# Half of a kernel's last matrix products as four 64x64 parts, with a changed order of evictions and stores

## The chip, the core and the metric

The kernel runs on one core of a Trainium2 chip. The core has five engines with queues of their own: PE (TensorE, matrix products; the profile shows its weight loads apart, as PEld), DVE (VectorE), ACT (ScalarE), POOL (GpSimd) and SP (SyncE, which here only issues DMAs). Matrix products land in PSUM[...]. The results of a product are copied ("evicted") from PSUM to SBUF by ACT or DVE and stored to HBM by DMA. The metric is the device time of one execution in microseconds.

## The reference

An input x of shape (4, 256, 64, 64), float32, passes through two layers. The first computes attention over the 49 positions of a dilated 7x7 neighbourhood: a 7x7 convolution to 128 channels, a 1x1 convolution to 49, a softmax over the 49, and with these weights a sum of the 49 shifted copies of x. The second layer is the one that the change touches. It whitens the channels in four groups of 64:

```
x = transpose(X, (1, 0, 2, 3)).reshape(g, nc, -1)      # g = 4 groups, nc = 64 channels
xc = x - mean
Sigma = EPS * I + einsum('gdm,gem->gde', xc, xc) / m
Sigma_N = Sigma * rTr                                   # rTr = 1 / trace
P = I
for _ in range(5):
    P3 = P @ P @ P
    P = 1.5 * P - 0.5 * P3 @ Sigma_N
wm = P * sqrt(rTr)
X_hat = wm @ xc                                         # per group
return X_hat * weight + bias
```

The last product takes a 64x64 matrix for each group of channels. It is followed by a scale and a shift for each channel.

## The kernel before, in words

The 256 channels are held as two blocks of 128 partitions (`cc` 0 and 1), each with two groups of 64 channels. An image's rows are held in two slots, even rows and odd rows (`slots[2 * b + pr]` for image `b` and row parity `pr`), each of (128, 2, 32, 64) for partition, channel block, row and column.

Most of the time goes to the first layer. Its convolution is done by evaluation and interpolation (products at lines 502 and 608). Both lines write 49 outputs each into two halves of the PE array's columns: `h = 0` to PSUM partitions from 0, `h = 1` to partitions from 64. The attention sum is at line 955, its transposes are at lines 926 and 987, and the sums for the covariance are gathered on the way at line 1008. Three slots that were spilled to HBM come back at line 880, queued on SP behind the last load of the attention weights (`bring_back`).

Then follows `whiten` (lines 1185 to 1260), a short serial chain for each channel block. The two chains are run in turn, step by step. It forms the covariance, runs the iteration with products at lines 1231 and 1238 and vector steps at line 1241, and ends with a scale for each channel (line 1251) and a shift: a one-column product (line 1255), then lines 1258 and 1259. Its whitening matrix `wm[cc]` is 128x128, with the matrices of two groups on the diagonal and zeros in the two other quarters.

The last stage (lines 1267 to 1298) applies it. For each image (3, 2, 1, 0), channel block and block of 8 rows per parity (`q`, 0 to 3), two products of 128x128 by 128x512 are made (line 1276), one for each row parity, into PSUM tiles of one bank from a pool of three (`tp()`). They are evicted alternately by ACT (line 1287) and DVE (line 1291), which apply scale and shift and interleave the two parities into an output tile `st` of 16 rows. After the second eviction SP stores the tile, 128 partitions of 4 KB (line 1295). There are four such tiles. In all the stage has 64 products, 64 evictions and 32 stores of 512 KB.

Work stands on each engine's queue in the order that a scheduling layer gives it at build time. `pe(...)` keeps products in the order of the program, `tc.high_priority()` moves work ahead. Waits between engines are put in by the layer: for data, and for the reuse of a buffer. PSUM tiles of the stage are `tp` (three banks). Elsewhere in the kernel there are `ps_y` (two banks, the sums of line 955) and `cv_buf` (two banks, the convolution); both lie unused during the last stage.

Of the kernel before, what the change touches and what calls it, by code (L numbers as in the profile page):

```python
# [9 lines left out]
F32 = mybir.dt.float32  # L10
AF = mybir.ActivationFunctionType
ALU = mybir.AluOpType
# [19 lines left out]
def kernel(  # L32
# [29 lines left out]
    nc = tc.nc  # L62
    B, C, H, W = x.shape
    P = 128
# [5 lines left out]
    SH, SW = H // 2, W // 2  # L70
# [4 lines left out]
    GW = 64  # L75
# [15 lines left out]
    def pe(ins):  # L91
        return tc.keep_in_program_order(ins)

    const = ctx.enter_context(tc.tile_pool(name="const", bufs=1))
    work = ctx.enter_context(tc.tile_pool(name="work", bufs=2))
# [3 lines left out]
    ps_y = ctx.enter_context(tc.tile_pool(name="ps_y", bufs=1, space=bass.MemoryType.PSUM))  # L99
    ps_sg = ctx.enter_context(tc.tile_pool(name="ps_sg", bufs=1, space=bass.MemoryType.PSUM))  # L100

    def tp():
        return ps_tp.tile([P, 512], F32, tag="tp", name="tp")


    ident = const.tile([P, P], F32, name="ident")
# [15 lines left out]
    slots = {}  # L122
    store = []
# [27 lines left out]
    t = tp()  # L151
# [3 lines left out]
    t = tp()  # L155
    nc.tensor.matmul(t[:, :1], w2T, b1_sb, start=True, stop=True)
    bias = const.tile([P, 1], F32, name="bias")
    nc.vector.tensor_tensor(bias, t[:, :1], b2_sb, ALU.add)

    cv_buf = []  # L160
    for k in range(2):
        t = ps_cv.tile([P, 512], F32, name=f"cv{k}")
# [53 lines left out]
    for k, c0 in enumerate(range(0, P, CB)):  # L216
        n = min(CB, P - c0)
        t = cv_buf[k % 2]
        for cc in range(NCC):
# [5 lines left out]
                    start=True, stop=True,  # L225
# [8 lines left out]
    for k0 in range(0, KT, TB):  # L234
        n = min(TB, KT - k0)
        t = tp()
# [906 lines left out]
    for b in range(1, B):  # L1143

        steps = []
        for r in range(len(ROWS)):
            k = NR0 + len(ROWS) * (b - 1) + r
# [16 lines left out]
                j += 1  # L1164
    apool.release()
    rpool = ctx.enter_context(tc.tile_pool(name="rp", bufs=1, reuse_waits="tile"))
    blk = rpool.tile([P, P], F32, name="blk")
    nc.gpsimd.memset(blk, 0.0)
    for g in range(P // GW):
# [10 lines left out]
    def square(name):  # L1180
        return bpool.tile([P, P], F32, tag="xb", name=name, bufs=4)

    wm, sc, beta = {}, {}, {}

    def whiten(cc):


        def evict(o, i):
            (nc.vector.tensor_copy if cc else nc.scalar.copy)(o, i)

        G = sig[:, cc]
        mu = work.tile([P, 1], F32, tag="mu", name=f"mu{cc}")
        nc.vector.tensor_scalar(mu, G[:, GW : GW + 1], 1.0 / NPIX, None, ALU.mult)
        D = square(f"D{cc}")
        nc.vector.tensor_scalar(D, ident, mu, None, ALU.mult)
        t = tp()
        nc.tensor.matmul(t[:, :P], blk, D, start=True, stop=True)
        nmu = work.tile([P, 1], F32, tag="nmu", name=f"nmu{cc}")
        nc.vector.tensor_scalar(nmu, mu, -1.0, None, ALU.mult)
        PS = rpool.tile([P, 2, P], F32, tag="PS", name=f"PS{cc}", bufs=2)  # L1200
        S = PS[:, 1]
        nc.vector.tensor_scalar(S, ident, EPS, None, ALU.mult)
        yield
        for g in range(P // GW):
            gs = slice(g * GW, (g + 1) * GW)
            nc.vector.scalar_tensor_tensor(
                S[gs, gs], G[gs, :GW], 1.0 / NPIX, S[gs, gs], ALU.mult, ALU.add
            )
        nc.vector.scalar_tensor_tensor(S, t[:, :P], nmu, S, ALU.mult, ALU.add)
        yield  # L1210
        dt_ = square(f"dt{cc}")
        nc.vector.tensor_tensor(dt_, S, ident, ALU.mult)
        dg = work.tile([P, 1], F32, tag="dg", name=f"dg{cc}")
        nc.vector.tensor_reduce(dg, dt_, AX.X, ALU.add)
        t = tp()
        nc.tensor.matmul(t[:, :1], blk, dg, start=True, stop=True)
        yield
        rtr = work.tile([P, 1], F32, tag="rtr", name=f"rtr{cc}")
        nc.vector.reciprocal(rtr, t[:, :1])
        nc.vector.tensor_scalar(S, S, rtr, None, ALU.mult)  # L1220


        i15 = square(f"i15_{cc}")
        nc.vector.tensor_scalar(i15, ident, 1.5, None, ALU.mult)
        Pm = PS[:, 0]
        nc.vector.scalar_tensor_tensor(Pm, S, -0.5, i15, ALU.mult, ALU.add)
        yield

        for it in range(1, T_ITERS):
            t = tp()  # L1230
            nc.tensor.matmul(
                t[:, : 2 * P], Pm, PS.rearrange("p a c -> p (a c)"), start=True, stop=True
            )
            sq = rpool.tile([P, 2, P], F32, tag="sq", name=f"sq{cc}_{it}", bufs=2)
            evict(sq.rearrange("p a c -> p (a c)"), t[:, : 2 * P])
            yield
            t = tp()
            nc.tensor.matmul(t[:, :P], sq[:, 0], sq[:, 1], start=True, stop=True)
            nc.vector.tensor_scalar(Pm, Pm, 1.5, None, ALU.mult)
            yield  # L1240
            nc.vector.scalar_tensor_tensor(Pm, t[:, :P], -0.5, Pm, ALU.mult, ALU.add)
            yield


        q = work.tile([P, 1], F32, tag="q", name=f"q{cc}")
        nc.scalar.activation(q, rtr, AF.Sqrt)
        qi = work.tile([P, 1], F32, tag="qi", name=f"qi{cc}")
        nc.vector.reciprocal(qi, q)
        nc.vector.scalar_tensor_tensor(q, qi, rtr, q, ALU.mult, ALU.add)
        scale = work.tile([P, 1], F32, tag="scale", name=f"scale{cc}")  # L1250
        nc.vector.scalar_tensor_tensor(
            scale, q, 0.5, gain_sb[:, cc : cc + 1], ALU.mult, ALU.mult
        )
        t = tp()
        nc.tensor.matmul(t[:, :1], Pm, mu, start=True, stop=True)
        yield
        bt = work.tile([P, 1], F32, tag="beta", name=f"beta{cc}")
        nc.vector.tensor_scalar(bt, t[:, :1], scale, -1.0, ALU.mult, ALU.mult)
        nc.vector.tensor_tensor(bt, bt, shift_sb[:, cc : cc + 1], ALU.add)
        wm[cc], sc[cc], beta[cc] = Pm, scale, bt  # L1260

    chains = [whiten(cc) for cc in range(NCC)]
    for _ in itertools.zip_longest(*chains):
        pass


    NT = 512
    TR = NT // W
    n = 0
    for b in (3, 2, 1, 0):  # L1270
        for cc in range(NCC):
            for q in range(SH // TR):
                st = rpool.tile([P, TR, 2, W], F32, tag="out", name=f"out_{b}_{cc}_{q}", bufs=4)
                for pr in range(2):
                    t = tp()
                    nc.tensor.matmul(  # L1276
                        t,
                        wm[cc],
                        slots[2 * b + pr][:, cc, q * TR : (q + 1) * TR, :].rearrange(
                            "p r w -> p (r w)"  # L1280
                        ),
                        start=True,
                        stop=True,
                    )
                    t3 = t.rearrange("p (r w) -> p r w", w=W)
                    if n % 2 == 0:
                        nc.scalar.activation(  # L1287
                            st[:, :, pr, :], t3, AF.Identity, bias=beta[cc], scale=sc[cc]
                        )
                    else:  # L1290
                        nc.vector.tensor_scalar(  # L1291
                            st[:, :, pr, :], t3, sc[cc], beta[cc], ALU.mult, ALU.add
                        )
                    n += 1
                nc.sync.dma_start(
                    out[b, cc * P : (cc + 1) * P, 2 * q * TR : 2 * (q + 1) * TR, :],
                    st.rearrange("p r two w -> p (r two) w"),
                )


# [29 lines left out]
```

## Time and profile before

| | |
|---|---|
| time, median of 14 runs | 766.55 us (762.0 to 777.28) |
| the profiled execution | 777.28 us, of it 775.5 us span on the core |
| mean granted clock of PE in it | 0.977 of full speed |
| PE busy | 717.0 us, 92% of the span |
| DVE, ACT, POOL busy | 623.9, 326.6 and 34.2 us |
| first and last record of a product at L1276 | start at 715.64, end at 770.82 us |
| evictions at L1287 (ACT) and L1291 (DVE) | 32 of 778 ns, 32 of 810 ns |
| stores at L1295 | 32 of 512 KB, median 2.6 us from issue to landing |
| last store issued | 771.73 us |

The profile shows one execution. L1276 is line 1276 of the kernel. A group of instructions has its busy time, the mean duration of one, and the idle time of the engine before it with the work that ended the wait. A float32 product shows as two weight loads and two matmul records. The records of matmuls that follow each other overlap[...]: a record is longer than the distance to the next one. The profiled execution is the slowest of the runs listed.

### The profile page before, as it was taken

Reading aid. Unit: us, or ns where it says so; the run is one execution under the profiler, and the core shown is the slowest. Engines: PE = TensorE matmul, PEld = TensorE weight load, DVE = VectorE, ACT = ScalarE, POOL = GpSimd, SP = SyncE. Lnnn points to the kernel's source line nnn. Section 1 sums busy time; section 2 is a strip of 40 time slices with the busy share of each in tenths; the row PEclk is TensorE's granted clock in tenths of the full one; section 3 lists DMA queues with packets and bytes.
Section 4 is the critical chain, followed back from the end, with each engine's and each line's share of the span. In section 5 each row is a group of like instructions: output and inputs, shape, how many; then the busy total and the mean of one; then the engine's idle time right before and its main releaser. Section 6 shows DMA issues by size and latency. Waiting matters only on the chain.

```text
span 775.5 us, 18389 instructions
## 1 busy us (share of the span) xinstructions
PE 717.0 (92%) x7444; PEld 547.6 (71%) x7444; DVE 623.9 (80%) x1302; ACT 326.6 (42%) x950; POOL 34.2 (4%) x46
## 2 busy tenths in 40 slices
PE   6969989959899999989999999999999889998997
PEld 1429564345798888679988966898898678885443
DVE  2739999999899999998997799799979765535443
ACT  2403241025455465355453443735435563322443
POOL 0410000030000020001000100000000000000000
PEclk9998999989899999999999999999999999999999
DMA  8991020041744385045743930442532143381676
GB/s 321 229 320 40 31 106 37 1 153 38 226 140 138 117 307 161 19 128 204 255 126 94 342 81 1 141 116 96 161 87 79 48 143 114 100 306 48 275 309 282
DMA packets 59773, 114.76 MB, mean 148 GB/s; under 512 B 22903, under 2 KB 42024, under 8 KB 58920
## 3 DMA queue, kind: packets, MB, share of 16 engines
q1 hardware_dynamic: 55992, 94.71, 36.9%
q0 software_dynamic: 3696, 18.88, 7.2%
q8 instruction: 59, 0.97, 0.5%
q14 instruction: 26, 0.21, 0.1%
HBM read 66.23 MB, written 47.33 MB: 146 GB/s over the span
## 4 chain that ended last, share of the span: by engine, by line
DVE 39%; PE 35%; issue 4%; ACT 4%; DMA 3%; SPq 1%; DVEq 0%; ACTq 0%
PE y L955 11%; PE cv L502 8%; PE tp L1276 7%; DVE xh L307 5%; DVE pv L307 3%; DVE rb L307 3%; DVE zz L307 3%; DVE ct L307 3%; PE sig L1008 3%; DVE ct L300 3%; PE tp L926 3%; PE tp L987 3%; DVE rb L300 2%; DVE pv L303 2%; DVE band L908 2%
## 5 line engine op out<-in xcount | busy, mean ns | idle before, releaser
L502 PE MATMUL cv<-xh,wr 128*49 128x128 f32 x4368 | 254.2, 278 | 17.6 <-DVE xh L300 14.7
L502 PEld LDWEIGHTS cv<-xh,wr 128*49 128x49 f32 x4368 | 248.1, 125 | 22.8 <-issue 12.4
L955 PE MATMUL y<-band,xb 128*128 128x224 f32 (+2 forms) x640 | 153.3, 379 | 12.9 <-ACT xb L934 8.2
L955 PEld LDWEIGHTS y<-band,xb 128*128 128x128 f32 x640 | 111.1, 195 | 34.5 <-ACT xb L934 10.5
L512 ACT COPY pv<-cv 113x486 f32<-113x486 f32 (+1 forms) x63 | 29.8, 475 | 79.3 <-PE cv L502 78.1
L974 ACT ACTIVATE slot<-y,pivot 128x512 f32<-128x512 f32 x53 | 36.7, 738 | 58.8 <-PE y L955 58.8
L995 ACT COPY yt<-tp 128x256 f32<-128x256 f32 x128 | 45.5, 378 | 35.1 <-PE tp L987 34.1
L926 PE MATMUL tp<-ident,slot 128*128 128x128 f32 x256 | 50.5, 300 | 7.2 <-ACT yt L995 7.2
L987 PE MATMUL tp<-ident,slot 128*128 128x128 f32 x256 | 51.8, 298 | 4.0 <-ACT xb L934 1.4
L908 DVE STREAM_TRANSPOSE band<-band 128x960 f32<-128x960 f32 (+1 forms) x48 | 50.8, 1059 | 5.1 <-DMA band<-sd 5.0
L987 PEld LDWEIGHTS tp<-ident,slot 128*128 128x128 f32 x256 | 41.3, 205 | 13.9 <-issue 4.5
L926 PEld LDWEIGHTS tp<-ident,slot 128*128 128x128 f32 x256 | 40.1, 206 | 14.7 <-ACT yt L995 9.1
L1291 DVE TENSOR_SCALAR out<-tp,scale,beta 128x512 f32<-128x512 f32 x32 | 25.9, 810 | 29.5 <-PE tp L1276 29.5
L857 ACT COPY zt<-d 32x112 f32<-32x112 f32 (+2 forms) x156 | 45.0, 288 | 1.7
L811 ACT ACTIVATE d<-tp,mx 128x49 f32<-128x49 f32 x128 | 37.1, 338 | 15.1 <-DVE mx L806 15.0
L1287 ACT ACTIVATE out<-tp,beta,scale 128x512 f32<-128x512 f32 x32 | 24.9, 778 | 32.0 <-PE tp L1276 32.0
L934 ACT COPY xb<-tp 128x256 f32<-128x256 f32 x87 | 30.4, 377 | 17.6 <-PE tp L926 16.9
L307 DVE SCALAR_TENSOR_TENSOR xh<-ct 128x512 f32<-128x512 f32 x42 | 27.7, 682 | 12.4 <-PE cv L502 12.2
L1008 PE MATMUL sig<-yt 128*64 128x65 f32 x1024 | 36.9, 225 | 0.0
L1008 PEld LDWEIGHTS sig<-yt 128*64 128x64 f32 x1024 | 32.4, 137 | 6.0 <-issue 4.5
L1276 PE MATMUL tp<-slot,PS 128*128 128x512 f32 x80 | 35.9, 593 | 0.0
L608 PE MATMUL cv<-slot,wi 128*49 128x496 f32 (+3 forms) x168 | 34.8, 571 | 0.0
(206 smaller groups left out, 982.4 us busy)
## 6 DMA issues: line engine op xcount, KB each, us to landing
out_dram<-out SPq DMA_DIRECT2D x32, 512.0 KB, 2.6
sd<-zt SPq DMA_DIRECT2D x16, 896.0 KB, 3.9
slot<-in_x_dram POOLq DMA_DIRECT2D x12, 1024.0 KB, 9.8
band<-sd SPq DMA_DIRECT2D x128, 84.0 KB, 2.1
wr<-gd SPq DMA_DIRECT2D x15, 588.0 KB, 3.9
wr<-gd SPq DMA_DIRECT2D x15, 490.0 KB, 3.5
spill<-slot POOLq DMA_DIRECT2D x3, 2048.0 KB, 8.2
back<-spill SPq DMA_DIRECT2D x3, 2048.0 KB, 8.1
```

What stands on the lines that cost most here:

```text
L300: return in_turn(TT(o, a, b, ALU.add))
L307: return in_turn(STT(o, a, f, b, ALU.mult, ALU.add))
L502: nc.tensor.matmul(cv[h * HB : h * HB + KT, k, sr : sr + n, sc : sc + n], wv[:, sc, sr, cc], xh[bc][:, :n, h * NCC + cc, :n], start=(j == ...
L811: nc.scalar.activation(d[:, h, i], lt[i // NI][:, i % NI, h, :KT], AF.Exp, bias=mx[:, i, h : h + 1], accum_out=s[:, h, i : i + 1],)
L857: ins = nc.scalar.copy(o, i)
L908: nc.vector.transpose(f, f)
L926: nc.tensor.transpose(t[:, cc * P : (cc + 1) * P], xt[:, cc, CR * m : CR * (m + 1), bass.ds(pc, SW, 2)], ident,)
L955: nc.tensor.matmul(ps[:, cc, q0 - half * HALF : q1 - half * HALF, :], xb[:, cc * P : (cc + 1) * P], rhs, start=(k == 0), stop=(k == len(PI ...
L987: nc.tensor.transpose(t[:, cc * P : (cc + 1) * P], yt[:, cc, CR * i : CR * (i + 1), bass.ds(pc, SW, 2)], ident,)
L995: nc.scalar.copy(yb.rearrange("p a g c -> p (a g) c")[:, :, :GW], t[:, :C].rearrange("p (e c) -> p e c", c=GW),)
L1008: nc.tensor.matmul(sig[g * GW : (g + 1) * GW, cc], yb[:, cc, g, :GW], yb[:, cc, g], start=(count[0] == 0 and cc == 0), stop=(count[0] == 4 ...
L1276: nc.tensor.matmul(t, wm[cc], slots[2 * b + pr][:, cc, q * TR : (q + 1) * TR, :].rearrange("p r w -> p (r w)"), start=True, stop=True,)
```

## The change

The stage now works on two blocks of 8 rows at a time (16 groups of four products). Of the four products of a group, the two of even rows are made as before, one bank each, from `tp()`; call them plain(0) and plain(1). The two of odd rows use that `wm` has only two non-zero quarters: each product is split into two of 64x64 by 64x512, so that a group has four such parts, for the four quarters of the array. For `k = 0` a channel group's result lands on its own partitions. For `k = 1` the two groups are exchanged: channels 0 to 63 land on PSUM partitions 64 to 127 and the other way round, so that each part has a quarter of its own. The two results `ts[0]` and `ts[1]` lie in two banks, which are in turn the two of `ps_y` and the two of `cv_buf`.

`ts[0]` is evicted whole. `ts[1]` is evicted in two halves of 64 partitions, each to the other 64 partitions of the output tile; its scale and shift come from `abx`, which holds them in exchanged order. `abx` is made by one small product per channel block at the end of `whiten`, with a permutation matrix `swap` that POOL writes earlier. `n[0]` counts evictions over all groups and alternates ACT and DVE: five in a group. The first store of a group follows when its 16 output rows are complete, the second at the end of the group. Output tiles are six instead of four.

```diff
+    swap = rpool.tile([P, P], F32, name="swap")
+    for g in range(P // GW):
+        nc.gpsimd.tensor_copy(
+            swap[:, g * GW : (g + 1) * GW], ident[:, (1 - g) * GW : (2 - g) * GW]
+        )
     blk = rpool.tile([P, P], F32, name="blk")
...
-        scale = work.tile([P, 1], F32, tag="scale", name=f"scale{cc}")
+        ab = work.tile([P, 2], F32, tag="ab", name=f"ab{cc}")
+        scale = ab[:, 0:1]
...
-        bt = work.tile([P, 1], F32, tag="beta", name=f"beta{cc}")
+        bt = ab[:, 1:2]
         nc.vector.tensor_scalar(bt, t[:, :1], scale, -1.0, ALU.mult, ALU.mult)
         nc.vector.tensor_tensor(bt, bt, shift_sb[:, cc : cc + 1], ALU.add)
         wm[cc], sc[cc], beta[cc] = Pm, scale, bt
+        yield
+
+        t = tp()
+        nc.tensor.matmul(t[:, :2], swap, ab, start=True, stop=True)
+        abx[cc] = work.tile([P, 2], F32, tag="abx", name=f"abx{cc}")
+        nc.vector.tensor_copy(abx[cc], t[:, :2])
...
+    n = [0]
+
+    def out_rows(o, i, scale, bias):
+        n[0] += 1
+        if n[0] % 2:
+            nc.scalar.activation(o, i, AF.Identity, bias=bias, scale=scale)
+        else:
+            nc.vector.tensor_scalar(o, i, scale, bias, ALU.mult, ALU.add)
+
+    def two_banks():
+        while True:
+            t = ps_y.tile([P, 2, NT], F32, tag="y", name="apply")
+            yield [t[:, k] for k in range(2)]
+            yield cv_buf
+
+    G0, G1 = slice(0, GW), slice(GW, P)
+    two = two_banks()
     for b in (3, 2, 1, 0):
         for cc in range(NCC):
-            for q in range(SH // TR):
-                st = rpool.tile([P, TR, 2, W], F32, tag="out", name=f"out_{b}_{cc}_{q}", bufs=4)
-                for pr in range(2):
-                    t = tp()
-                    nc.tensor.matmul(t, wm[cc], ...)
...
+            for q in range(0, SH // TR, 2):
+                st = [
+                    rpool.tile([P, TR, 2, W], F32, tag="out", name=f"out_{b}_{cc}_{q + k}", bufs=6)
+                    for k in range(2)
+                ]
...
+                ts = next(two)
+
+                def plain(k):
                     t = tp()
+                    pe(nc.tensor.matmul(t, wm[cc], y[0][k], start=True, stop=True))
+                    out_rows(st[k][:, :, 0, :], rows_of(t), sc[cc], beta[cc])
...
+                plain(0)
+                for k in range(2):
+                    for i in (G0, G1):
+                        o = i if k == 0 else (G1 if i is G0 else G0)
+                        pe(
+                            nc.tensor.matmul(
+                                ts[k][o], wm[cc][i, i], y[1][k][i],
+                                start=True, stop=True, skip_group_check=True,
+                            )
                         )
...
+                out_rows(st[0][:, :, 1, :], rows_of(ts[0]), sc[cc], beta[cc])
+                store(0)
+                for i, o in ((G1, G0), (G0, G1)):
+                    out_rows(
+                        st[1][o][:, :, 1, :], rows_of(ts[1])[i], abx[cc][i, 0:1], abx[cc][i, 1:2]
+                    )
+                plain(1)
+                store(1)
```

More of the change, by code (lines that the diff above doesn't have):

```diff
@@ L1181, in square @@
         return bpool.tile([P, P], F32, tag="xb", name=name, bufs=4)
-    wm, sc, beta = {}, {}, {}
+    wm, sc, beta, abx = {}, {}, {}, {}
     def whiten(cc):
@@ L1268 @@
     TR = NT // W
-    n = 0
+    n = [0]
[11 more added lines that the diff above has]
+    G0, G1 = slice(0, GW), slice(GW, P)
@@ L1270 @@
+    two = two_banks()
     for b in (3, 2, 1, 0):
         for cc in range(NCC):
-            for q in range(SH // TR):
-                st = rpool.tile([P, TR, 2, W], F32, tag="out", name=f"out_{b}_{cc}_{q}", bufs=4)
-                for pr in range(2):
-                    t = tp()
[L1276 to L1283, printed above, removed]
-                    )
[L1285 to L1288, printed above, removed]
-                        )
[L1290 to L1298, printed above, removed]
@@ new lines, with store @@
+            for q in range(0, SH // TR, 2):
[3 more added lines that the diff above has]
+                ]
+                y = [
+                    [
+                        slots[2 * b + pr][:, cc, (q + k) * TR : (q + k + 1) * TR, :].rearrange(
+                            "p r w -> p (r w)"
+                        )
+                        for k in range(2)
+                    ]
+                    for pr in range(2)
+                ]
+                rows_of = lambda t: t.rearrange("p (r w) -> p r w", w=W)
+                ts = next(two)
+                def plain(k):
+                    t = tp()
+                    pe(nc.tensor.matmul(t, wm[cc], y[0][k], start=True, stop=True))
+                    out_rows(st[k][:, :, 0, :], rows_of(t), sc[cc], beta[cc])
+                def store(k):
+                    nc.sync.dma_start(
+                        out[
+                            b, cc * P : (cc + 1) * P, 2 * (q + k) * TR : 2 * (q + k + 1) * TR, :
+                        ],
+                        st[k].rearrange("p r two w -> p (r two) w"),
+                    )
+                plain(0)
[7 more added lines that the diff above has]
+                            )
+                        )
+                out_rows(st[0][:, :, 1, :], rows_of(ts[0]), sc[cc], beta[cc])
[3 more added lines that the diff above has]
+                        st[1][o][:, :, 1, :], rows_of(ts[1])[i], abx[cc][i, 0:1], abx[cc][i, 1:2]
+                    )
+                plain(1)
+                store(1)
```

## The prediction

> **What bounds the kernel now.** I read the chain that ended last first, then the timeline of its last stretch, then the sums of that stage, then the sizes of its instructions. The tail of the chain in order of time (start, us, engine, line):
>
> ```profile
> 708.11 1.74 PE tp L1231 x4
> 715.78 55.05 PE tp L1276 x128
> ```
>
> One stage, the 64 whitening products, is the last 55 us, and PE alone carries it. The waits and groups of that stage (busy us, mean ns, idle before it and who ended it):
>
> ```profile
> L1276 PE MATMUL tp<-slot,PS 128*128 128x512 f32 x80 | 35.9, 593 | 0.0
> L1291 DVE TENSOR_SCALAR out<-tp,scale,beta 128x512 f32<-128x512 f32 x32 | 25.9, 810 | 29.5 <-PE tp L1276 29.5
> L1287 ACT ACTIVATE out<-tp,beta,scale 128x512 f32<-128x512 f32 x32 | 24.9, 778 | 32.0 <-PE tp L1276 32.0
> L1276 PE MATMUL tp<-back,PS 128*128 128x512 f32 x48 | 22.1, 592 | 0.0
> ```
>
> PE is never idle; both evicting engines idle more than half the time, always for PE. A product is two records ("passes"): 80 + 48 = 128 for 64 products. Next, the sums of two windows: the reload of spilled slots, then this stage (last columns: PE clock, share of DMA, GB/s).
>
> ```profile
> 690.00:694.00 4.00, 3.69 (x31) 3.24 (x28) 1.87 (x4) 1.44 (x4) 0.00 (x0) 1.00 1.02 434
> 716.00:771.00 55.00, 54.82 (x128) 23.94 (x126) 25.49 (x35) 24.88 (x32) 0.00 (x0) 1.00 0.70 288
> ```
>
> The stores use 0.70 of the DMA engines; full load moved 434 GB/s. The clock is 1.00, so the stage scales to other executions. 55.0 us for 128 passes is 0.429 us a pass, 0.858 a product.
>
> Whether PE can do several small products at once, and what a change of array shape costs, is in the timeline of earlier stretches (start, duration):
>
> ```profile
> 28.73 0.32 PE L239 MATMUL tp<-ident,tapT 113*128 113x113 f32 x1 [0.17 <-ACT tap L214]
> 28.97 0.64 PE L608 MATMUL cv<-slot,tap 128*49 128x512 f32 x2
> ...
> 299.87 0.40 PE L502 MATMUL cv<-xh,wr 128*49 128x128 f32 x4
> 300.20 0.39 PE L987 MATMUL tp<-ident,slot 128*128 128x128 f32 x1
> ```
>
> At 28.97 two 512-column passes into two 64-column halves of the array ran inside 0.64 us, 7 ns apart. The page's L608 row (168 passes, 34.8 us busy) says the same: 0.207 us a pass for a mean of 488 columns, half of what one array-wide pass needs. So two column halves run fully side by side, both passes of each. The switch: the 113-column pass at 28.73 streams for 113/512 x 0.429 = 0.095 us, yet the next starts 0.246 later; before other L502 groups it is 0.106 beyond the stream. I take 0.11 going in. Coming back, the last L502 pass starts at 299.99 (0.40 us record less its 0.275), streams 0.107, and L987 starts at 300.20: 0.10.
>
> [...] Nothing in this trace splits the array by rows[...]. [...]
>
> **The change, part by part.** The changed stage has 16 groups of four products: plain(0), two products as four 64x64 parts, plain(1).
>
> *PE per group.* plain(0): 2 x 0.429 = 0.858. Switch in 0.106. Four parts, if at once: 2 passes, 0.858, plus 3 starts of 7 ns, plus 0.04 since the first pass after a switch shows its weight load (467 against 429 ns between the first two L608 pairs): 0.918. Switch out 0.098. plain(1): 0.858 + 0.084, the delay of the second pass that the first L1276 product shows (513 against 429 ns). Sum 2.922 us instead of 4 x 0.858 = 3.433. The parts save 0.86 of 3.43, the switches give back 0.33. Sixteen groups: 46.75 instead of 54.93 us, **-8.2**. The switch costs for the 64x64 shape aren't in the trace: between nothing (5.3 us better) and twice (5.3 worse); I take the column-half values, the nearest.
>
> *Before the stage.* In the compiled order both swap products stand ahead of the first plain product in PE's queue and wait for beta. Now the first L1276 starts at 715.64; L1259 ends at 716.10 and 716.23. Then 0.05 to PE, two one-column products at the 0.22 us that L1255 took before the next weights, and weights: first product at about 716.64, **+1.0**. All 64 products queue behind it. The two abx copies (about 0.2 us each) end before DVE's first eviction. The swap tile costs POOL two copies; POOL is empty in this stage, they can run some 90 us earlier. Uncovered they would cost a fraction of a us. The larger pool leaves the three reloads on SP with the same waits.
>
> *Evictions.* 80 instead of 64. In the compiled order over two groups A and B, ACT does A plain(0), A plain(1), A first half, B ts[0], B second half; DVE does A ts[0], B plain(0), A second half, B first half, B plain(1). Halves have half the partitions but 512 elements each: I take 0.78 and 0.81 as for whole ones. Five cost 3.9 and 4.05 us of a 5.84 us pair. With results readable 0.63 to 0.68 us after their last pass starts, I place them (us from the pair's start): ACT 1.1-1.9, 3.1-3.9, 3.9-4.7, 5.0-5.8, 6.5-7.3; DVE 2.1-2.9, 4.0-4.8, 4.8-5.6, 5.6-6.4, 6.4-7.2. The bank pair of A is wanted again at 6.8 and free at 5.6; that of B at 9.7 and free at 7.3. PE never waits, with 1.2 us to spare; without that cover 16 x 0.8 / 2 = 6.4 us would appear.
>
> *Stores.* Same 32 of 512 KB, but bunched: in SP's order A's second stands behind B's first, so issues fall at 2.9, 5.85, 6.25 and 7.33 of each pair. A 4 KB packet took 159 ns and each of 16 engines has 8 a store: 1.27 us, 5.1 us a pair of 5.84: hidden while it runs, 0.87 of the engines.
>
> *The end.* Now the last pass starts at 770.23, its eviction ends 771.67, the last store is issued 1.08 us after PE's last stream and lands 2.63 later. Changed: half and plain(1) of B end 7.3 into a pair whose PE ends at 5.84, so issue is 0.4 later; and two stores stand ahead, their packets ending 9.3, where this store's own could begin at 8.2: **+1.4** in all.
>
> Sum: -8.2 + 1.0 + 1.4 = **-5.8 us**. The profiled execution (span 775.5, time 777.28) would become 769.7 and 771.5. It lies 10.7 above the median of the 14 runs, 766.55; the stage ran at full clock, so I take the difference to the median: **760.8 us**.
>
> **The rivals.** *Two pairs in turn (ends slower).* Only two parts stream at once, as the column halves do in this trace, because splitting by rows adds nothing for float32. The four-part block is then 4 passes, 1.78 instead of 0.918; a group 3.78 us, above the old 3.43, the stage 60.5: +5.6 + 1.0 + 0.6 for the end (less bunching) = 773.8. For it: no row split in the trace[...]. Against: the column halves interleave both passes perfectly. It decides where the block exceeds 0.918 + 5.8/16 = 1.28 us.
> *Staggered.* PE takes each part's second pass before the third part may start: three pass times, 1.35; group 3.35, gain 1.3, lost again to the 2 us around it: 767.2, no change. Against it: L608's pairs don't stagger.
> *The stores become the bound.* 16.78 MB at the 344 GB/s that this stage shows in its best slices is 48.8 us from the first packet at about 720.4: last landing 769.6 instead of 774.4, 761.8. Against: 434 GB/s when more was queued.
> *Eight passes one after another* (no overlap at all): block 3.5, about 803.
>
> **How the numbers follow.** Four at once 0.67 (760.8, own range 758 to 764), stores bound 0.07, staggered 0.09, two pairs 0.14, no overlap 0.03. Faster by over 0.2% (about what a measurement of this kernel can tell from no change): the first two, 0.73 after some loss to the same; within 0.2%: 0.10; slower 0.17. The range runs from 757 (switches nearly free, about -3.8) to 768.5 (switches twice as dear, 766.1, and the staggered case with its error); it leaves out the pairs and worse, 0.17.
>
> **What would show it.** Right: groups of four 512-column passes whose starts lie some 7 ns apart and two such sets 0.47 us apart; plain(0) to plain(0) of the next group 2.92 us; PE still without idle time; the stage's DMA share 0.82 or more; first whitening product 1.0 us later after the last vector step of the iteration (now L1241) than now; last store landing 5.1 us after PE's last stream against 3.7. Wrong: four-part blocks over 1.28 us; PE waiting for ACT or DVE at the four-part products; stores landing over 4 us after issue in mid-stage.

## The result and the profile after

The changed kernel takes **761.22 us** (median of 10 runs, 760.1 to 764.76) against 766.06 us of the kernel before in the same comparison (48 runs). The ratio is 0.9943, with a 95% interval of 0.9929 to 0.9958. The forecast was 760.8 us. The profiled execution of the changed kernel took 760.1 us, with a span of 758.3. The profiled execution of before is a slow one (777.28 us) and was 11.7 us later already at line 880, so the two spans are not compared, only the stage, which in both ran at a granted clock of 1.00.

The chain that ended last, its tail (start, us, engine, line):

```profile
739.44 1.91 PE tp L1324 x4
742.37 1.91 PE tp L1324 x4
745.31 1.91 PE tp L1324 x4
748.24 1.93 PE tp L1324 x4
```

L1324 is now a plain product. The rows are one group apart: 2.93 us, predicted 2.922. PE alone still carries the stage. Its groups from 705 us on (busy us, mean ns, idle before and who ended it):

```profile
L1324 PE MATMUL tp<-slot,PS 128*128 128x512 f32 x32 | 16.1, 621 | 0.0
L1293 DVE TENSOR_SCALAR out<-tp,ab 128x512 f32<-128x512 f32 x16 | 13.0, 811 | 8.9 <-PE tp L1324 8.6
L1291 ACT ACTIVATE out<-tp,ab 128x512 f32<-128x512 f32 x16 | 12.4, 778 | 11.5 <-PE tp L1324 6.0 <-ACT out L1291 5.4
L1340 PE MATMUL apply<-slot,PS 64*64 64x512 f32 x48 | 6.5, 614 | 0.0
L1291 ACT ACTIVATE out<-apply,abx 64x512 f32<-64x512 f32 x8 | 6.2, 774 | 0.2
```

PE's column of idle time is 0.0 in both of its rows, and the groups keep their distance of 2.93 us to the end: no product waited for a bank (here the PSUM tile that one 128x512 result goes to). The last row prices what the trace of before could not: evicting 64 partitions takes as long as evicting 128 (774 against 778 ns).

The first group, and how the stage begins, in the timeline (start, duration):

```profile
703.82 0.38 PE L1262 MATMUL tp<-mu,PS 128*128 128x1 f32 x2
...
704.38 0.27 DVE L1266 TENSOR_TENSOR ab<-ab,shift_sb 128x1 f32<-128x1 f32 x2
704.58 0.61 PE L1271 MATMUL tp<-ab,swap 128*128 128x2 f32 x4 [0.38 <-DVE ab L1266]
...
705.05 1.10 PE L1324 MATMUL tp<-slot,PS 128*128 128x512 f32 x2
706.08 0.66 PE L1340 MATMUL apply<-slot,PS 64*64 64x512 f32 x4
```

Two things are in it. The first passes of all four parts (x4) stand in one record of 0.66 us, where four passes one after another would need 4 x 0.43 = 1.7; singly they start at 706.084, 706.091, 706.097 and 706.104. And the first plain product (705.05) stands behind the swap products (L1271), 1.23 us behind the second one-column product (703.82). Before, that distance was 0.25 us:

```profile
715.39 0.38 PE L1255 MATMUL tp<-mu,PS 128*128 128x1 f32 x2 [0.16 <-DVE PS L1241]
715.64 1.96 PE L1276 MATMUL tp<-slot,PS 128*128 128x512 f32 x4
```

The sums of stretches of the stage, and the landing times of the stores, complete it (last columns of the first: PE clock, DMA share, GB/s):

```profile
716.00:740.00 24.00, 24.00 (x98) 7.38 (x99) 16.74 (x21) 15.99 (x21) 0.00 (x0) 1.00 0.88 358
740.00:752.00 12.00, 12.00 (x50) 3.45 (x48) 8.34 (x12) 8.03 (x11) 0.00 (x0) 1.00 0.89 363
```

```profile
L1328 SPq DMA_DIRECT2D out_dram<-out x32: 332/333/1662, 708.1 to 753.6; - x32
...
DMA to landing us min/median/max: 2.6/3.4/5.2
```

The DMA share is up from 0.70 to 0.88. A store takes a median of 3.4 us to land against 2.6, up to 5.2 in mid-stage, and one issue took SP 1.66 us instead of 0.33. The prediction named landings over 4 us as a sign that stores had become a bound. The sign came, but PE waited for nothing: at 0.88 of the DMA engines the stores were not the bound.

The stage in one sum: from the first to the last pass 46.59 us (705.05 to 751.64) against 54.59 (715.64 to 770.23), **-8.0**; start +0.98; from the last pass's start to the span's end 6.69 us against 5.27, **+1.42**. Together -5.60. From the end of the last record of line 1008, ahead of the whitening chain, to the span's end it is 68.71 us against 74.35: -5.64 (the chain itself has the other -0.04). The medians differ by 4.8 (3.2 to 5.4 by the interval). The 0.8 us between that and the stage's sum is not explained by these two profiled executions.

### The profile page after: what moved, and what is told of

It reads as the page before. It is cut to its first block, busy times and chain, and to the rows that moved or that the text cites. A ratio compares the mean times of both kernels' runs of the same rounds, so it can differ in the third digit from the quotient of the medians.

```text
span 758.3 us, 18542 instructions
## 1 busy us (share of the span) xinstructions
PE 705.8 (93%) x7512; PEld 534.4 (70%) x7512; DVE 630.7 (83%) x1312; ACT 332.6 (44%) x958; POOL 34.5 (5%) x48
## 4 chain that ended last, share of the span: by engine, by line
DVE 38%; PE 37%; ACT 5%; issue 4%; DMA 3%; SPq 1%; DVEq 0%; ACTq 0%
PE y L955 11%; PE cv L502 10%; DVE xh L307 4%; PE tp L1324 4%; DVE pv L307 3%; DVE zz L307 3%; PE tp L987 3%; PE sig L1008 3%; PE tp L926 3%; DVE ct L307 3%; DVE ct L300 2%; DVE rb L307 2%; DVE rb L300 2%; DVE pv L303 2%; DVE band L908 2%
## 5 line engine op out<-in xcount | busy, mean ns | idle before, releaser
L502 PE MATMUL cv<-xh,wr 128*49 128x128 f32 x4368 | 251.5, 276 | 8.7 <-DVE xh L300 5.6
L502 PEld LDWEIGHTS cv<-xh,wr 128*49 128x49 f32 x4368 | 245.4, 124 | 13.8 <-issue 11.5
L934 DVE COPY xb<-tp 128x256 f32<-128x256 f32 x41 | 16.5, 422 | 22.2 <-PE tp L926 22.2
L307 DVE SCALAR_TENSOR_TENSOR pv<-pv 113x162 f32<-113x162 f32 x105 | 33.6, 320 | 1.0
L811 ACT ACTIVATION_READ_ACCUMULATOR d<-tp,mx 128x1 f32 x128 | 30.5, 240 | 0.0
```

The source lines that it names most:

```text
L307: return in_turn(STT(o, a, f, b, ALU.mult, ALU.add))
L502: nc.tensor.matmul(cv[h * HB : h * HB + KT, k, sr : sr + n, sc : sc + n], wv[:, sc, sr, cc], xh[bc][:, :n, h * NCC + cc, :n], start=(j == ...
L811: nc.scalar.activation(d[:, h, i], lt[i // NI][:, i % NI, h, :KT], AF.Exp, bias=mx[:, i, h : h + 1], accum_out=s[:, h, i : i + 1],)
L934: (nc.vector.tensor_copy if tail else nc.scalar.copy)(xb, t[:, :C])
```

## The experiments

Each kernel is the changed kernel with one edit, unless said otherwise. The kernel before was timed again beside them; its medians were 765.65 us (experiments 1 to 4), 765.53 (5 to 8) and 765.42 (9 and 10).

**1. The same stage with whole products.** All but the parts stays: two banks, five evictions a group, six tiles, the swap product. The second tile's halves go to their own partitions, since nothing is exchanged.

```diff
 for k in range(2):
-    for i in (G0, G1):
-        ...
-        pe(nc.tensor.matmul(ts[k][o], wm[cc][i, i], y[1][k][i], ...))
+    pe(nc.tensor.matmul(ts[k], wm[cc], y[1][k], ...))
```

> The changed kernel with the four 64x64 parts of a group put back as two whole 128x128 products into the same banks; five evictions a group, exchange product, six output tiles and stores stay. My theory (the parts are the gain): 64 products of 0.858 us again, plus 1.0 us for the exchange products and some 0.7 us for the bunched last stores: 767 to 768.5 us, 0.2% slower than the kernel before. Rival (the gain is from the new evictions, stores or buffers): stays near 761 us.

Measured: 769.28 us (768.12 to 771.24), ratio 1.0053 (1.0035 to 1.0072). So by the medians everything around the parts costs 3.6 us against before, where 1.7 were expected (1.0 for the swap, 0.7 at the end). The trace separates the causes. From the last record of line 1008 to the end it has 78.70 us against 74.35 before, 4.35 more. The start has 0.98 of that, as in the changed kernel, and the end 0.72 (5.98 against 5.27): together the expected 1.7. The other 2.65 fall where this one execution had a lower clock: the stage takes 56.28 us from first to last pass against 54.59 (+1.70), and the whitening chain ahead of it 15.20 against 14.25 (+0.95; its stretch at half clock is 6.9 us long instead of 3.5). The stretch in the stage (last columns: clock, DMA share, GB/s):

```profile
705.00:725.00 20.00, 19.96 (x46) 9.05 (x47) 9.22 (x14) 8.83 (x12) 0.00 (x0) 0.91 0.51 210
```

The parts alone are worth 769.28 - 761.22 = 8.1 us by the medians. By the traces, without the low-clock stretches, they are worth 78.70 - 2.65 - 68.71 = 7.34 us: 8.0 in the stage, less the 0.7 by which the end of the changed kernel is longer. That the medians give nearly the 8.2 of the prediction is thus in part chance; the stage's 8.0 is what answers to it.

**2. Two at a time instead of four.** Each product is split by columns only: 128 rows, 64 columns. Four of these make the two products, each two at once. This has the changes of array shape (the switches of the prediction) and no gain from rows.

```diff
-                ts[k][o], wm[cc][i, i], y[1][k][i],
+                ts[k][i], wm[cc][:, i], y[1][k],
```

> The two odd-row products of a group split by columns alone: four products of 128 rows by 64 columns, so that only two can be in the array at once. It pays both switches of array shape per group and saves nothing. My theory: four passes 1.72 us plus 0.33 us for the switches, group 3.77 instead of 3.43 us, so 5.4 us above the run with whole products, 772 to 774 us. If splitting by rows were not what gains, it would be near 761 us; if switches were free, near 767.5.

Measured: 774.96 us (771.36 to 776.32), ratio 1.0120 (1.0094 to 1.0145). It is the rival "two pairs in turn" made on purpose, and it lands near where that was worked out (773.8). The timeline (start, duration):

```profile
738.19 1.02 PE L1324 MATMUL tp<-back,PS 128*128 128x512 f32 x2
739.14 1.94 PE L1339 MATMUL apply<-slot,PS 128*64 128x512 f32 x8
741.01 1.98 PE L1324 MATMUL tp<-back,PS 128*128 128x512 f32 x4
```

The block of parts takes 741.01 - 739.14 = 1.87 us where the four-part block takes 1.02 (706.08 to 707.10). So what the rows add is shown, and so is the switch: the step from experiment 1 is 5.7 us over 16 groups, 0.36 a group. The trace of the changed kernel says the same: in 0.523 from the last plain pass (705.561) to the first part instead of 0.429, out 0.539 from the first of the parts' second passes to the plain one, and the second plain pass comes 0.104 late; the two sets of passes of the parts start 0.480 apart, 0.05 late: 0.094 + 0.110 + 0.104 + 0.051 = 0.36. Predicted, over the same four terms, were 0.106 + 0.119 + 0.084 + 0.04 = 0.35 (0.119 with the three starts of 7 ns).

**3. Half the switches.** Each image and channel block (eight products) is one run: plain(0), the parts of two groups (two bank pairs), then three plain products. Eight output tiles.

```diff
+            plain(0)
+            for h in range(2):
+                ts.append(next(two))
+                for k in range(2):
+                    for i in (G0, G1):
+                        ...
+            for h in range(2):
+                if h:
+                    plain(2)
+                ...
+                plain(2 * h + 1)
+                store(2 * h + 1)
```

> The parts of two groups stand next to each other in the tensor engine's queue (8 parts, then plain products), so that there are 8 switches into the quarters instead of 16; eight output tiles. My theory: 8 x 0.33 = 2.7 us less than the changed kernel, 758.5 us (757.5 to 759.5), the evictions still hidden. Rival: evictions are already what sets the pace, no gain: 761 us.

Measured: 756.85 us (754.23 to 758.59), ratio 0.9881 (0.9853 to 0.9909), 4.4 us below the changed kernel's median. The trace shows only part of that. The chain's steps are 5.55 to 5.60 us for eight products (730.39 to 735.99 to 741.59), against 2 x 2.93 = 5.87: 2.1 to 2.5 us over eight blocks, somewhat less than eight switches in and out at 0.36 (2.9). The end is 0.3 shorter (6.37 us against 6.69). The rest is not explained; the interval is 4.3 us wide. The whole of this profiled execution can't settle it, since it too has a stretch at half clock at the start of the stage: from the last record of line 1008 to its end it takes 68.71 us, as long as the changed kernel.

**4. All products as parts.** Then there is no switch at all, and a bank pair is evicted as two whole ones. Three pairs of banks take turns (`ps_y`, `cv_buf`, two of `tp`). Of two output tiles one has its channel groups exchanged; it is stored by two DMAs of 64 partitions, which put them right.

```diff
+                out_rows(st[1][:, :, pr, :], rows_of(ts[1]), abx[cc][:, 0:1], abx[cc][:, 1:2])
...
+                for g in range(P // GW):
+                    c0 = cc * P + (1 - g) * GW
+                    nc.sync.dma_start(
+                        out[b, c0 : c0 + GW, rows(1), :], flat[1][g * GW : (g + 1) * GW]
+                    )
```

> All 64 products as parts, no plain ones. Both row parities of the second tile of a group land with the two channel groups exchanged, are evicted whole (64 evictions instead of 80) and exchanged back by the store, two DMAs of 64 partitions. Tensor engine 32 blocks of 0.87 us = 28 us; evictions 64 x 0.8 / 2 = 26 us; stores 32 x 1.27 us = 41 us, which become the bound. My theory: first packets some 4.1 us after the first part, then 40.7 us and 0.4: 45 us from first part to last landing instead of 52, so 754.5 us (753.5 to 757), DMA share near 1.0 in the stage. Rival (more DMAs or some other limit): 758 us or more, DMA share under 0.9.

Measured: 765.2 us (759.8 to 770.14), ratio 0.9994 (0.9975 to 1.0013). A miss by 10.7 us. The waits of the stage (in total, times, longest) and two of its stretches:

```profile
DVE out L1293 <- DMA out_dram<-out: 18.3, 11, 2.7
ACT out L1291 <- DMA out_dram<-out: 17.9, 11, 2.4
```

```profile
720.00:740.00 20.00, 14.98 (x100) 4.64 (x104) 9.18 (x12) 9.75 (x14) 0.00 (x0) 0.91 0.96 325
740.00:752.00 12.00, 8.35 (x62) 2.33 (x56) 5.55 (x8) 5.03 (x8) 0.00 (x0) 1.00 0.98 332
```

Here the rival "the stores become the bound" is real: both evicting engines wait for output tiles, the DMA engines are full, and yet move only 325 to 332 GB/s. The mean packet of 4 KB took 191 ns instead of 159. Whether that was the price of stores of 64 partitions or of any stores in a row was open, and experiment 7 asks it.

**5. The swap later.** The two swap products go behind the first group's parts.

```diff
-        t = tp()
-        nc.tensor.matmul(t[:, :2], swap, ab, start=True, stop=True)
...
+                for k in range(NCC) if n[0] == 1 else ():
+                    t = tp()
+                    pe(nc.tensor.matmul(t[:, :2], swap, abs_[k], start=True, stop=True))
```

> The two products that swap the groups of the constants move in TensorE's order from ahead of the first plain product to behind the first group's four parts. If they cost what the prediction says (+1.0 us, paid once, since all 64 products queue behind them), the first whitening product starts 0.5 to 1.0 us after the second correction product (1.23 in the changed kernel, 0.25 in the kernel before), and the time is 0.5 to 1.0 us below the changed kernel's 761.2: about 760.4. Rival: the swap is hidden and the 0.98 us has another cause (the constants themselves come later); then the first product stays 1.2 us behind and the time is the same.

Measured: 760.45 us (759.25 to 760.79), ratio 0.9939 (0.9918 to 0.9961). The timeline decides:

```profile
703.47 0.38 PE L1262 MATMUL tp<-mu,PS 128*128 128x1 f32 x2 [0.16 <-DVE PS L1247]
703.68 0.30 PEld L1319 LDWEIGHTS tp<-slot,PS 128*128 128x128 f32 x2
703.71 1.10 PE L1319 MATMUL tp<-slot,PS 128*128 128x512 f32 x2
```

The first plain product is back at 0.24 us behind the one-column product: the +0.98 was the swap, all of it. Not all of it is gained: the two swap products now stand inside the first group, which takes 3.38 us instead of 2.93. That leaves 0.98 - 0.45 = 0.53 us. (The whole of this execution does not show it: its whitening chain took 15.23 us instead of 14.21, with the longer stretch at half clock of experiment 1.) The median moved by 0.8, inside the intervals.

**6. Evictions and stores in the order of the program.** The scheduling layer is kept from reordering evictions, which also parts the bunched stores.

```diff
-            nc.scalar.activation(o, i, AF.Identity, bias=bias, scale=scale)
+            pe(nc.scalar.activation(o, i, AF.Identity, bias=bias, scale=scale))
         else:
-            nc.vector.tensor_scalar(o, i, scale, bias, ALU.mult, ALU.add)
+            pe(nc.vector.tensor_scalar(o, i, scale, bias, ALU.mult, ALU.add))
```

> Evictions kept in the order of the program, so the two stores of a pair of groups that fell together in the changed kernel (issued 2.9, 5.85, 6.25 and 7.33 us into each pair) are issued at 2.9, 4.6, 5.85 and 7.1. If the tail of 5.14 us after TensorE's last stream comes from two stores standing ahead of the last one, as the prediction says, the last landing is 3.7 to 4.1 us after the last stream and the time is about 1.3 us below the changed kernel: 759.9. The landings over 4.5 us in mid-stage go too. Rival: the tail is the price of any last store at this DMA load; then it stays near 5 us and the time is the same, 761.

Measured: 760.46 us (755.45 to 761.82), ratio 0.9933 (0.9908 to 0.9958), again 0.8 below the changed kernel, too little for the medians to show. The stores of its trace:

```profile
L1328 SPq DMA_DIRECT2D out_dram<-out x32: 332/332/751, 704.6 to 749.9; - x32
...
DMA to landing us min/median/max: 2.6/2.6/4.9
```

The median landing is back at 2.6 us at the same DMA share (0.90 in mid-stage), so bunching made it 3.4. From the last pass's start (748.08) to the span's end it is 5.57 us, against 6.69 in the changed kernel and 5.27 before: of the +1.42 at the end, 1.12 came from the order of evictions and stores. The last store shows which part is which. It is issued 1.78 us after the last pass's start (1.97 in the changed kernel, 1.51 before), and from its issue to the end it takes 3.79 us (4.72 and 3.76): the bunched stores ahead of it were 0.93. Single landings of 4.9 stay, against expectation.

**7. Experiment 4 with whole stores.** It leaves out the exchange of channel groups of every second tile; nothing else differs. Theory A puts the loss of experiment 4 on its stores of 64 partitions, theory B on stores of any form.

```diff
-                for g in range(P // GW):
-                    ...
+                nc.sync.dma_start(out[b, cc * P : (cc + 1) * P, rows(1), :], flat[1])
```

> As the kernel in which all 64 products are parts (765.2), but each second tile is stored by one DMA of 128 partitions instead of two of 64. It leaves out the exchange of the two channel groups of every second tile, which the two DMAs did on the way. Theory A: that kernel lost its gain[...]: then packets of 4 KB come back from a mean of 190 ns to 159, the stores move 400 GB/s or more at full share, and the time is 765.2 - 6 to 765.2 - 9: 756 to 759. Theory B: the stores of this stage can't be sustained above some 330 GB/s whatever their form: the mean packet stays near 190 ns and the time within 2 us of 765.

Measured: 754.88 us (2 runs, 754.58 and 755.18), ratio 0.9866 (0.9833 to 0.9899). The stretch that answers to that of experiment 4:

```profile
720.00:740.00 20.00, 15.88 (x122) 5.00 (x118) 10.80 (x15) 10.97 (x16) 0.00 (x0) 1.00 1.03 417
```

The same bytes at 417 GB/s, and the mean packet is back at 159.7 ns. So the 10 us lost in experiment 4 were the form of the store, half of its bytes going out 64 partitions at a time. (Two smaller DMAs in the place of one come with that form; the two are not separated.) Why that form moves less was not shown. An estimate from the two means: 191 ns a packet with half of the bytes in stores of 64 partitions, and 159.7 ns with none, give about 222 ns for a packet of those stores, 1.4 times as long, if the packets of whole stores stayed at 159.7.

**8. All parts, the exchange undone by eviction.** Experiment 7, but `ts[1]` is evicted in two halves, as in the changed kernel; of a block's three evictions ACT does one and DVE two, or the reverse, in the order of the program.

```diff
+                    out_rows(pr, st[0][:, :, pr, :], rows_of(ts[0]), sc[cc], beta[cc])
+                    for i, o in ((G1, G0), (G0, G1)):
+                        out_rows(
+                            1 - pr, st[1][o][:, :, pr, :], rows_of(ts[1])[i],
+                            abx[cc][i, 0:1], abx[cc][i, 1:2],
+                        )
```

> All 64 products as four parts at once, the exchanged halves put right by evicting each half by itself (96 evictions instead of 80, two of three of a block on one engine), all stores of 128 partitions. TensorE needs 32 x 0.87 = 28 us; evictions 16 x (3 x 0.81 = 2.43) = 39 us on VectorE; stores 16.78 MB at 413 GB/s = 40.6 us. If a store of 128 partitions keeps 159 ns a packet, the stores bound the stage: first store about 3.3 us after the first product, 40.6 us of packets, 2 us to land: 46 us against 52 in the changed kernel, 755 us or a little less. If stores of any form are held to 330 GB/s: 51 + 5 = 56 us, 765 us.

Measured: 765.08 us (763.16 to 766.74), ratio 0.9999 (0.9986 to 1.0013). Neither case: the packet is 159.2 ns and the DMA share only 0.79. Its waits:

```profile
PEld apply L1330 <- ACT out L1290: 23.6, 10, 3.0
DVE out L1292 <- ACT out L1290: 12.6, 6, 2.4
PE apply L1330 <- DVE out L1292: 10.5, 7, 2.2
```

The evictions are the bound, by waiting for each other: DVE's half of an `apply` pair waits until ACT has read the other bank (ACT ends at 726.77 us, DVE starts at 726.80). `cv_buf` shows no such wait: ACT's halves start at 726.79, before DVE reads the other bank at 728.47. In the kernel the two banks of `apply` are one tile and those of `cv_buf` are two, so the likely reason is that the layer that puts in waits goes by tiles.

**9. Experiments 3 and 5 together.**

```diff
             ts = []
             plain(0)
             ...
+            for k in range(NCC) if not abx else ():
+                t = tp()
+                pe(nc.tensor.matmul(t[:, :2], swap, abs_[k], start=True, stop=True))
+                ...
             for h in range(2):
```

> The kernel with half the switches (756.85) with the two swap products behind its first parts. If what moving them saved in the other kernel (about 0.8 us) adds up: 756.1 us, first whitening product about 0.4 us after the second correction product. Rival: the stores hold this kernel already, 0.93 of the DMA engines in its late stretch, so an earlier start only queues stores earlier: 756.9, no change against it.

Measured: 756.61 us (755.6 to 759.43), ratio 0.9891 (0.9864 to 0.9917). The first product starts 0.24 us after the one-column product; the median is 0.2 us from that of experiment 3, and whether the 0.8 was gained cannot be told at these intervals. Its trace, with a clock of 1.00 all through the stage, is a better measure of the two edits together: from the last record of line 1008 to the end 65.41 us against 68.71 in the changed kernel, 3.3 us less, where the medians differ by 4.6.

**10. One engine for a block.** Experiment 8 with all three evictions of a block on one engine, blocks in turn, the swap later, and eight tiles.

```diff
-                            1 - pr, st[1][o][:, :, pr, :], rows_of(ts[1])[i],
+                            pr, st[1][o][:, :, pr, :], rows_of(ts[1])[i],
```

> All 64 products as four parts at once, with 128-partition stores, as in the kernel with separately evicted halves (765.1), but all three evictions of a block of four parts on one engine, the engines taking blocks in turn, eight output tiles, and the swap products later. Theory: that kernel lost to ACT and DVE waiting for each other at the shared two-bank tile (12.6 + 5.3 us of such waits in its stage); without them evictions need 32 x 3 x 0.80 / 2 = 38.4 us and stores 40.6 us of packets, so the last landing is 46 to 48 us after the first product, against 52.2 in the changed kernel: 755 to 757, and 753 if the start is 0.8 us earlier as well. The wait of one of them for the other falls below 3 us. Rival: TensorE waits for bank sets, since a set is taken for 0.9 + 0.3 + 2.4 = 3.6 us and comes round in 3 x 1.2 = 3.6; if each block slips by 0.3 us the stage is 10 us longer: 763.

Measured: **754.75 us** (753.45 to 757.02), ratio 0.9863 (0.9837 to 0.9888). It beats both kernels by its interval. Its waits and stretches:

```profile
PEld apply L1325 <- ACT out L1285: 7.6, 5, 1.7
PEld apply L1325 <- PE tp L1325: 7.6, 5, 1.5
```

```profile
720.00:736.00 16.00, 13.09 (x111) 4.19 (x101) 15.46 (x21) 14.90 (x20) 0.00 (x0) 1.00 1.02 414
736.00:748.00 12.00, 5.63 (x44) 1.70 (x40) 9.71 (x12) 8.07 (x11) 0.00 (x0) 0.90 1.02 414
```

The waits of ACT and DVE for each other, 12.6 and 5.3 us in experiment 8, are gone from the list. The eight tiles are a second difference, but no eviction of experiment 8 waited for a tile; the later swap is worth about 0.5 us (experiment 5). In the first stretch DVE and ACT are busy 15.46 and 14.90 of 16 us and the DMA engines are full at 414 GB/s: PE, the bound of the kernel before, now has idle time, and the evictions and the stores are both near their limit. From the first product to the span's end it is 48.4 us (703.15 to 751.6), against 53.3 in the changed kernel.

## Why the prediction was right

*The group.* 2.922 us predicted, 2.933 measured. Its terms: the four parts run at once, 7 ns apart. Before the result that was the author's estimate: the trace of before shows two column halves side by side, but no split by rows. Experiment 2 shows the rows' share (a block of 1.02 us for 1.87) and experiment 1 that the gain is the parts', 8.0 us in the stage for 8.2. The choice that carried it was to take the column-half switch for the 64x64 one: in 0.094 for 0.106, out 0.110 for 0.119 (with the 7 ns starts), the second pass of a plain product 0.104 late for 0.084, the second set of passes of the parts 0.051 late for 0.04. Single terms are off by up to a quarter, in both directions, so that their sum (0.36 for 0.35) is closer than they are. Bounds from nothing to twice were wider than needed.

*The start.* +1.0 predicted, +0.98 in the trace; experiment 5 shows that it is the order of the swap products.

*The end.* +1.4 predicted, +1.42 in the trace. The prediction had the last store issued 0.4 us later and held up by two stores ahead of it; 0.46 later and 0.96 of hold-up were measured. By experiment 6, 1.12 goes when evictions and stores keep the order of the program, so the mechanism is shown for that part; the remaining 0.30 is nearly all the later issue.

*Evictions.* 0.78 and 0.81 us for half the partitions were a guess; 772 to 774 and 804 to 818 ns were measured. PE never waited for a bank, as placed (0.0 us idle at lines 1324 and 1340). The swap on POOL and the reloads cost nothing that the trace shows: POOL's two copies took 0.41 us at 596.2 us, 108 us before their use, and the reloads land in 8.0 us against 8.1.

*Stores.* 0.87 of the engines predicted, 0.88 and 0.89 measured, hidden as said. What was off is the sign: landings over 4 us were listed as a mark of a wrong forecast, but they held up nobody here. Bunching made the median landing 3.4 us instead of 2.6 (experiment 6); it is not the cause of every long one, since single landings of 4.1 us stand in the trace of before and of 4.9 in experiment 6.

*The rivals.* Two pairs in turn, staggered and no overlap fall with the 7 ns. The rival of the stores did not decide here, and its price was misjudged: it took 344 GB/s as a limit, where whole stores sustain 414 to 417 (experiments 7 and 10).

*From stage to time.* -5.8 was carried to the median; the profiled executions gave -5.64, the medians -4.8, and the interval of the ratio ends at -5.4. The step "I take the difference to the median" is thus off by about 1 us. Its reason was that the stage ran at full clock in the one execution seen, and that does not hold of all: experiments 1, 2 and 3 have some 3.4 us at about half clock at the start of the stage. Whether that makes the difference here is open, since the other executions of both kernels have no trace. That the time itself was met to 0.4 us is partly luck: the median of before came out 0.5 us lower in the comparison than in the 14 runs, which offset half of the 1 us.

## What to carry to other kernels

Block-diagonal weights of 64x64 use a quarter of the array each, and four such parts did run at once here (7 ns apart, a block of 1.02 us where two at a time took 1.87); price each change of array shape (0.36 us in and out here) and gather parts into long runs: halving the switches brought another 2.1 to 2.5 us in the stage's steps, 4.4 by the medians. When PE speeds up, look next at evictions by partitions (half the partitions cost the same time here, 774 against 778 ns on ACT), at two engines reading one tile (12.6 and 5.3 us of waits in experiment 8), and at the form of the stores: with half of the bytes in stores of 64 partitions, 325 to 332 GB/s instead of 417, experiment 4 lost the whole gain. Small products that feed later evictions belong behind the first large ones (about 0.5 us here).

## What the runs showed of the hardware that was not expected

- An eviction of 64 partitions by 512 elements took as long as one of 128: 772 to 774 ns against 778 on ACT, 804 to 818 against 809 to 811 on DVE.
- Stores of 128 partitions of 4 KB sustained 414 to 417 GB/s at full share (1.02 to 1.03 in experiments 7 and 10), 159 to 160 ns a packet; with half of the bytes in stores of 64 partitions it was 325 to 332 GB/s and a mean of 191 ns.
- SP's issue of a DMA, mostly 0.33 us, took up to 1.66 us in the changed kernel, at a DMA share of 0.88 to 0.89. Full DMA engines alone do not do that: in experiment 10, at a share of 1.02, no issue took over 0.34 us. What does is open. The issues of experiment 10 from 720 us on (ns, min/median/max):

```profile
L1344 SPq DMA_DIRECT2D out_dram<-out x11: 332/332/333, 720.9 to 746.1; - x11
L1343 SPq DMA_DIRECT2D out_dram<-out x10: 332/332/333, 721.8 to 744.4; - x10
```

- In the profiled executions of experiments 1, 2 and 3 the granted clock was 0.50 to 0.53 for some 3.4 us at the start of the stage (0.89 to 0.91 over its first 16 to 20 us in 1 and 3); the changed kernel and experiments 5, 6 and 9 had 1.00 there. In experiment 1 the stage was 1.7 us longer for that, and the chain ahead of it, with 6.9 us at half clock instead of 3.5, by 0.95. A stage of one execution is compared with another only after a look at its clock.
